# Preparing a selective scan's delta and delta u: where the copies, the constant and the units on GpSimd are put

## The chip, the cores and the metric

The kernel runs on one core of a Trainium2 chip. The metric is the device time of one launch in microseconds (us), lower is better. A core has five engines with queues of their own: TensorE (PE in the profile, with its weight loads as PEld), VectorE (DVE), ScalarE (ACT), GpSimd (POOL) and SyncE (SP), which here only issues the transfers. Each takes its instructions in order; semaphores tie them together.

## The reference

Four layers, each x + ss2d(group_norm(x)), over eight images of 48 x 48 positions and 96 channels. Of one layer, what matters here is the selective scan over 192 inner channels, 16 states and four directions (rows, columns, and both backwards):

```python
x_dbl = jnp.einsum('bkdl,kcd->bkcl', xs, x_proj_weight)
dts, Bs, Cs = jnp.split(x_dbl, [R, R + N], axis=2)
dts = jnp.einsum('bkrl,kdr->bkdl', dts, dt_projs_weight)
A = -jnp.exp(A_logs.astype(jnp.float32)).reshape(K, Din, N)
delta = jax.nn.softplus(dts + dt_projs_bias.reshape(K, Din)[None, :, :, None])
...
def step(h, inp):
    u, dl, Bv, Cv = inp
    dA = jnp.exp(dl[..., None] * A)
    h = h * dA + (dl * u)[..., None] * Bv[:, :, None, :]
    y = jnp.einsum('bkdn,bkn->bkd', h, Cv)
    return (h, y)
```

Around it stand an input projection, a depthwise 3 x 3 convolution with SiLU before, a layer norm, a gate with SiLU and an output projection behind. Layer 3 sums its decays in another way (a cumulative sum divided by the decay); the kernel gives it a short path of its own, over the ends of the sequence alone.

## The kernel before, in words

**Chunks and units.** Layers 0 to 2 run over four pairs of images, and each pair over 12 groups: three tiles of channels, two orders of the positions (ph), two directions (d). A group of 2304 positions is cut into 3 chunks of 768. That makes 432 chunks. A chunk is worked off in 16 units n; one unit has 128 partitions, which are 64 channels for each of two states. A unit needs, over its 768 positions: the decay exp(delta a), made by ScalarE (`exp`, L764); delta u times B; the scan h = decay h + delta u B on VectorE (L798); h times C on GpSimd (L807); and the sum over states on TensorE into a PSUM accumulator (`add_up`, L854).

**Two kinds of units.** In ten units of a chunk the rows of B are spread over the partitions by four bf16 matmuls from `brow` into a PSUM tile `b` of a pool of two (`spread`, L667), and VectorE multiplies them with delta u (L794) ahead of the scan. In the other six (`pooled`, L711) a transfer brings B already spread into the tile `bb`, GpSimd multiplies it with delta u (`weigh`, L741), and ScalarE's decay goes into the PSUM tile `b` instead; VectorE then has the scan alone. The transfer of `bb` is issued five turns ahead of its unit and `weigh` three.

**Delta of the next chunk.** While a chunk runs, `prepare` (L580) makes the delta of the next, in two halves of 384 positions: a matmul from the rank to the channels (L603); |x|, relu, exp(-|x|) on ScalarE (L611 to L613); ln(1 + e), 1 + e and 1 - (1 + e) (L615 to L617); and eight matmuls with identity matrices that sum e, 1 - (1 + e), the logarithm and the relu in a PSUM bank v (L623). The pair e and 1 - (1 + e) adds what 1 + e lost in rounding. Then `to_twins` (L574) copies delta from v into both halves of the partitions with four copies on ScalarE (L578), VectorE multiplies v by u in place (`times_u`, L631 or, with strided columns, L634), and four more copies take delta u out of v. Each `yield` ends a step of `prepare`, and one step is made in each turn.

**The order.** There is no scheduler: the order on each engine is that in which the loop of `run` issues. Turn k issues, for unit k: the transfers ahead, `spread` of unit k + 1 (or its exponential into PSUM), `weigh` and the exponential of unit k + 3, the copy of the last unit's carry, the product and scan of unit k, the product with C; then one step of `prepare` and one step of side work (`beside`: the convolution and projections of the next pair, or the epilogue of the last), and `add_up` of unit k - 2. When a chunk's accumulator is finished, it is copied out by ScalarE (L871), and the next one begins with four matmuls (`begin_sum`, L839) ahead of the sum of unit 1; a chunk that turns from forwards to backwards keeps its accumulator. In the turn in which an accumulator is copied out, `beside` comes before `add_up`. Two turns after a chunk's first unit no side step is made.

A `spread` needs a buffer of `b`, so it waits for the scan of two units before. TensorE takes it in order, and VectorE's product waits for it.

**Rows of B.** `load` (L743) fetches `brow`, 2 x 48 rows of bf16, with the transfers of a chunk's first unit, four turns ahead.

## Time and profile before

| | |
|---|---|
| median of 3 runs | 20515.53 us (20514.31 to 20521.39) |
| the profiled execution's own time | 20509.65 us |
| its span, first to last instruction | 20507.7 us |
| mean granted TensorE clock | 0.904 |
| busy DMA engines, 1000 to 18000 us | 0.83 to 0.87 in windows of 1000 us |
| product with C on POOL, three forms over 768 positions | 1.815 to 1.817 us |
| product with B on POOL | 1.819 us, 2592 of them |
| product with B on DVE | 0.946 us, 4320 of them |
| scan on DVE | 1.739 to 1.814 us, 6912 of them |
| exponential on ACT | 0.901 to 0.931 us, 6912 of them |
| a 64 x 384 copy on ACT | 0.473 us, 2 x 3456 of them |
| 1 - (1 + e) on ACT, L617 | 0.615 us, 864 of them over 384 positions |
| product with u on DVE | 0.543 us (L631) and 0.814 us (L634), 432 each |

A row of the profile's groups names line, engine, operation, output and inputs with shapes, count, busy time and the mean of one; "idle before" is time in which the engine stood ahead of such an instruction, with what ended it. In the view of waits each row reads: who waited, for whom, total us, times, longest. Busy times of engines that overlap say little of the end; what counts is which wait ends last. Layers 0 to 2 take the first 18500 us; layer 3's short path the rest.

### The profile page before, as it was taken

What the parts mean: (1) busy time and instruction counts of PE and PEld (TensorE: products, weight loads), DVE (VectorE), ACT (ScalarE), POOL (GpSimd) and SP (SyncE); (2) the same over time, 40 slices, a digit from 0 to 9 for tenths busy, and PEclk for the clock granted to TensorE, in tenths of its full rate; (3) what the DMA queues carried; (4) which work ended last, traced back from release to release, by engine and by line L of the source; (5) the groups of instructions that cost most, each with busy time, mean ns of one, the idle gap of its engine ahead of it and who ended that gap; (6) DMA issues with size and microseconds to landing.
All of it is one profiled execution on the core that took longest, in us unless ns stands there. A gap on an engine that the chain in (4) does not pass through costs nothing. (4 is left out here: it accounts for less than half of the span.)

```text
span 20507.7 us, 304889 instructions
## 1 busy us (share of the span) xinstructions
PE 17283.2 (84%) x88322; PEld 7546.6 (37%) x88322; DVE 17656.0 (86%) x14161; ACT 16243.7 (79%) x30020; POOL 17768.2 (87%) x10121
## 2 busy tenths in 40 slices
PE   8888888888888888888888888888888888888886
PEld 2323333333333333333333333333333333335565
DVE  5999999999999999999999999989989989995543
ACT  5777887887887887887877887877877877877776
POOL 5999999999999999999999999999999999995432
PEclk8998998998998999998998999988988998999997
DMA  5888888888888888888888888888888888883221
GB/s 147 223 221 222 219 220 224 222 219 221 220 225 222 219 229 221 221 229 219 221 228 220 217 225 219 218 218 220 217 219 219 220 219 222 219 220 109 76 72 51
DMA packets 1963444, 4200.13 MB, mean 205 GB/s; under 512 B 369456, under 2 KB 720048, under 8 KB 1948592
## 3 DMA queue, kind: packets, MB, share of 16 engines
q1 hardware_dynamic: 1961776, 4180.52, 77.8%
q8 instruction: 726, 11.89, 0.3%
q14 instruction: 942, 7.72, 0.2%
HBM read 4026.64 MB, written 152.27 MB: 204 GB/s over the span
## 5 line engine op out<-in xcount | busy, mean ns | idle before, releaser
L807 POOL TENSOR_TENSOR cb<-cb,da 128x768 f32<-128x768 f32 x4320 | 7831.3, 1817 | 799.5 <-issue 258.3
L854 PE MATMUL acc<-cb,twin 128*64 128x384 f32 x27648 | 7018.1, 542 | 663.6 <-POOL cb L807 660.3
L798 DVE TENSOR_TENSOR_SCAN da<-da,carry,b 128x768 f32<-128x768 f32 x2880 | 5223.3, 1814 | 176.4 <-ACT b L764 2.3
L741 POOL TENSOR_TENSOR bb<-bb,du 128x768 f32<-128x768 f32 x2592 | 4714.0, 1819 | 361.0 <-DMA bb<-xd 207.8
L794 DVE TENSOR_TENSOR b<-du,b 128x768 f32<-128x768 f32 x4320 | 4087.6, 946 | 883.9 <-PE b L667 785.4
L807 POOL TENSOR_TENSOR cb<-cb,bb 128x768 f32<-128x768 f32 x2592 | 4705.1, 1815 | 155.0 <-DVE bb L798 57.1
L667 PE MATMUL b<-brow,pick 96*64 96x512 bf16 (+2 forms) x18816 | 2761.6, 355 | 1787.6 <-DVE da L798 1408.4
L764 ACT ACTIVATE da<-dl,a 128x768 f32<-128x768 f32 x4320 | 4013.6, 931 | 245.8 <-POOL cb L807 214.0
L854 PEld LDWEIGHTS acc<-cb,twin 128*64 128x64 f32 x27648 | 2268.9, 150 | 3089.4 <-issue 1400.3
L798 DVE TENSOR_TENSOR_SCAN bb<-b,carry,bb 128x768 f32<-128x768 f32 x1728 | 3109.0, 1799 | 114.8 <-ACT b L764 53.5
L764 ACT ACTIVATE b<-dl,a 128x768 f32<-128x768 f32 x2592 | 2334.4, 901 | 590.2 <-DVE da L798 558.4
L798 DVE TENSOR_TENSOR_SCAN da<-da,b 128x768 f32<-128x768 f32 x1440 | 2525.4, 1754 | 85.6 <-DVE b L794 0.9
L667 PEld LDWEIGHTS <-pick 96*64 96x64 bf16 x18816 | 974.1, 114 | 4192.1 <-DVE da L798 2506.3
L578 ACT COPY dl<-ps 64x384 f32<-64x384 f32 x3456 | 1635.3, 473 | 756.7 <-PE ps L623 720.7
L312 PE MATMUL ps<-pad,diag 128*128 128x480 f32 (+1 forms) x4320 | 2165.7, 599 | 11.5 <-DVE eyc L1087 9.9
L623 PE MATMUL ps<-du,cst 128*64 128x384 f32 (+1 forms) x7296 | 1709.7, 516 | 93.1 <-ACT du L617 77.0
L578 ACT COPY du<-ps 64x384 f32<-64x384 f32 x3456 | 1635.7, 473 | 190.0 <-DVE ps L634 91.2
L798 DVE TENSOR_TENSOR_SCAN bb<-b,bb 128x768 f32<-128x768 f32 x864 | 1502.2, 1739 | 94.9 <-ACT b L764 40.5
L623 PE MATMUL ps<-dl,cst 128*64 128x384 f32 (+1 forms) x7296 | 1412.4, 483 | 0.0
L312 PEld LDWEIGHTS ps<-pad,diag 128*128 128x128 f32 x4320 | 687.5, 191 | 1211.4 <-issue 1090.1
L603 PE MATMUL ps<-dts,w 6*128 6x384 f32 (+5 forms) x2432 | 946.3, 595 | 176.1 <-DMA dts<-xd 103.7
L611 ACT ACTIVATE du<-ps,w 128x384 f32<-128x384 f32 (+1 forms) x912 | 521.4, 572 | 622.3 <-PE ps L603 611.5
(144 smaller groups left out, 19159.8 us busy)
## 6 DMA issues: line engine op xcount, KB each, us to landing
cb<-xd SPq DMA_DIRECT2D x13952, 192.0 KB
bb<-xd SPq DMA_DIRECT2D x5184, 192.0 KB
brow<-xb SPq DMA_DIRECT2D x864, 72.0 KB
yd<-y SPq DMA_DIRECT2D x48, 1152.0 KB
ey<-yd SPq DMA_DIRECT2D x256, 216.0 KB
cb<-xd SPq DMA_DIRECT2D x128, 384.0 KB
ex<-xs SPq DMA_DIRECT2D x256, 108.0 KB
xd<-xt SPq DMA_DIRECT2D x32, 684.0 KB
```

Of the source, the lines that this page charges most:

```text
L312: nc.tensor.matmul(ps[:, :m], ly.diag[:, int(t == 2), j, :], pad[:, r0 + dy : r0 + dy + nr, dx : dx + W], start=(j == 0), stop=(j == 8),)
L578: nc.scalar.copy(z[64 * h : 64 * h + 64, g, at], v[64 * g : 64 * g + 64])
L603: nc.tensor.matmul(o[:, :m], ly.dtw[q0 : q0 + r, k, chans], dts[q0 : q0 + r, at], start=True, stop=True,)
L611: nc.scalar.activation(e, v, AF.Abs, bias=bias)
L623: nc.tensor.matmul(v[half], ident[:, half], z1, start=(i == 0), stop=(i == 3))
L667: nc.tensor.matmul(o[64 * h : 64 * h + 64], pick[:, b, n : n + 1].to_broadcast([2 * NR, 64]), rows, start=True, stop=True,)
L741: nc.gpsimd.tensor_mul(b, b, self.du[n % 2])
L764: nc.scalar.activation(da, self.dl[n % 2], AF.Exp, scale=layers[self.l].a2[:, int(self.t == 2), n % 2, k, i : i + 1],)
L794: nc.vector.tensor_mul(b, self.du[n % 2], b)
L798: nc.vector.tensor_tensor_scan(way(h), way(da), way(b), start, ALU.mult, ALU.add)
L807: nc.gpsimd.tensor_mul(c, c, h)
L854: nc.tensor.matmul(self.acc[64 * g : 64 * g + 64, a, : self.m // 2], twin, c[:, a, :], start=False, stop=(pair + 2 == NS and not self.turns),)
```

## The change

It has four parts.

1. `prepare` no longer makes 1 - (1 + e) on ScalarE. A bf16 matrix with ones in its first row and zeros elsewhere, times a column of ones, puts the constant 1 in v with two matmuls over 384 columns; -(1 + e) is added by a negated identity (`less`, in the place of a constant that is no longer used by then).
2. The four copies of delta stay. `times_u` comes one turn after them, in the first half of a chunk as in the second, and writes `du` in SBUF. Three copies within SBUF then bring delta u into both halves of the partitions.
3. The units with B on GpSimd are 2, 4, 7, 9, 12 and 15 in place of 2, 5, 7, 10, 13 and 15.
4. `brow` of the next chunk is fetched in turn 6, ten units ahead, where the next chunk belongs to the same layer and pair.

```diff
+    less = cst[:, P : 2 * P]
+    unit = cpool.tile([P, 64], BF16, name="unit")
+    nc.gpsimd.memset(unit, 0.0)
+    nc.gpsimd.memset(unit[0:1], 1.0)
+    unit_row = cpool.tile([P, 1], BF16, name="unit_row")
+    nc.gpsimd.memset(unit_row, 1.0)
...
+    nc.scalar.activation(less, ident, AF.Copy, scale=-1.0)
...
-            nc.scalar.activation(w1, w1, AF.Identity, bias=ones, scale=-1.0)
             yield
             v = bank()[:, :m]
-            for i, z1 in enumerate((e, w1, lg, x)):
+            for g in range(2):
+                nc.tensor.matmul(
+                    v[64 * g : 64 * g + 64], unit, unit_row.to_broadcast([P, m]),
+                    start=True, stop=False,
+                )
+            for w, z1 in ((less, w1), (ident, e), (ident, lg), (ident, x)):
                 for g in range(2):
                     half = slice(64 * g, 64 * g + 64)
-                    nc.tensor.matmul(
-                        v[half], ident[:, half], z1, start=(i == 0), stop=(i == 3)
-                    )
-                if i % 2 == 1:
+                    nc.tensor.matmul(v[half], w[:, half], z1, start=False, stop=(z1 is x))
+                if z1 is e or z1 is x:
                     yield
...
-            to_twins(dl, at, v)
+            for g in range(2):
+                for h in range(2):
+                    nc.scalar.copy(dl[64 * h : 64 * h + 64, g, at], v[64 * g : 64 * g + 64])
             if z + m == c.m:
                 if l == NLAYER - 1:
                     c.sum_up()
                 c.ready = True
+            yield
+            times_u(du[:, 0, at])
+            yield
+            for h in (1, 0):
+                nc.scalar.copy(du[64 * h : 64 * h + 64, 1, at], du[64:P, 0, at])
+            nc.scalar.copy(du[64:P, 0, at], du[0:64, 0, at])
+            if z + m < c.m:
                 yield
-            times_u(v)
-            yield
-            to_twins(du, at, v)
-            yield
...
-            return n in (2, 5, 7, 10, 13, 15) and self.l < NLAYER - 1
+            return n in (2, 4, 7, 9, 12, 15) and self.l < NLAYER - 1
...
+            if n == 6 and coming_to < len(chunks):
+                z = chunks[coming_to]
+                if (z.l, z.p) == (l, p):
+                    z.load_rows()
```

`load_rows` holds the lines that were in `load` and returns at once where the rows have been fetched.

The steps of `prepare` fall on other turns. First half: matmuls of the sum in turns 2 and 3 as before, delta's copies in turn 4, the product with u behind unit 5 (before: unit 4), delta u's copies in turn 6 (before: 5). Second half: the matmul from the rank in turn 7 (6), the sum in 10 and 11 (9 and 10), delta's copies in 12 (11), the product with u behind unit 13 (12), delta u's copies in turn 14 (13).

More of the change, by code (lines that the diff above doesn't have):

```diff
@@ L572, in load_dt @@
             )
-    def to_twins(z, at, v):
-        for g in range(2):
-            for h in range(2):
-                nc.scalar.copy(z[64 * h : 64 * h + 64, g, at], v[64 * g : 64 * g + 64])
     def prepare(c):
@@ L741, in weigh, with load_rows @@
                 nc.gpsimd.tensor_mul(b, b, self.du[n % 2])
+        def load_rows(self):
+            if self.brow is not None:
+                return
+            self.brow = rpool.tile([2 * NR, SCAN], BF16, name="brow", tag="brow")
+            for j, b in enumerate(range(2) if self.t == 2 else (self.t, self.t)):
+                nc.sync.dma_start(
+                    self.brow[NR * j : NR * j + NR, : self.m],
+                    state[self.l, self.p]["xb"][
+                        self.ph, b, :, self.d, :, self.c0 : self.c0 + self.m
+                    ],
+                )
         def load(self, n):
-            s, m, at = state[self.l, self.p], self.m, slice(self.c0, self.c0 + self.m)
             if n == 0:
-                self.brow = rpool.tile([2 * NR, SCAN], BF16, name="brow", tag="brow")
-                for j, b in enumerate(range(2) if self.t == 2 else (self.t, self.t)):
-                    nc.sync.dma_start(
-                        self.brow[NR * j : NR * j + NR, :m],
-                        s["xb"][self.ph, b, :, self.d, :, at],
-                    )
+                self.load_rows()
             self.cb[n] = cb = cbpool.tile([P, SCAN], F32, name="cb", tag="cb")
```

## The prediction

> **What bounds the kernel now.** I read the page first (its busy line and slices), then the waits of each engine between 1000 and 18500 us, where layers 0 to 2 run, and then the timeline of one chunk.

> ```profile
> PE 17283.2 (84%) x88322; PEld 7546.6 (37%) x88322; DVE 17656.0 (86%) x14161; ACT 16243.7 (79%) x30020; POOL 17768.2 (87%) x10121
> ...
> POOL 5999999999999999999999999999999999995432
> PEclk8998998998998999998998999988988998999997
> ```

> No engine is alone at its limit. Layers 0 to 2 are 432 chunks of 16 units. From scan end to scan end in the trace, a chunk takes 42.5 us. POOL's own work for it is 16 products with C and 6 with B, 22 x 1.816 = 40.0 us; DVE's is 10 units at about 2.7 us (product and scan, back to back), 6 at 1.75 (scan alone) and two products with u (0.55 or 0.81 each), some 39 us, and about 0.7 for norms. So 3 us of a chunk are waits between engines; only these can be won or lost in layers 0 to 2. Which waits DVE has:

> ```profile
> DVE b L794 <- PE b L667: 745.4, 702, 5.9
> DVE ps L634 <- ACT dl L578: 112.7, 109, 3.6
> DVE bb L798 <- ACT b L764: 90.8, 63, 3.3
> DVE b L794 <- PE acc L854: 85.4, 34, 4.8
> DVE ps L631 <- ACT dl L578: 84.1, 94, 3.5
> ```

> The columns are total us, times, longest. The window holds 412 chunks, so DVE waits 1.8 us a chunk for TensorE's rows of B (`spread`, L667), 0.48 for ScalarE's delta copies before it may multiply by u in place (L631, L634), 0.22 for an exponential. By unit, the first kind stands before unit 11 (0.67 us a chunk on average) and unit 1 (0.50); before units 3, 4 and 6 it is under 0.15.

> The next view is TensorE's timeline where units 1 to 6 of one chunk go by:

> ```profile
> 6022.51 0.52 PE L667 MATMUL b<-brow,pick 96*64 96x512 bf16 x4
> 6022.85 0.81 PE L854 MATMUL acc<-cb,twin 128*64 128x384 f32 x4
> 6023.50 1.46 PE L623 MATMUL ps<-du,cst 128*64 128x384 f32 x8
> 6024.79 0.49 PE L667 MATMUL b<-brow,pick 96*64 96x512 bf16 x4
> 6025.12 1.46 PE L623 MATMUL ps<-dl,cst 128*64 128x384 f32 x8
> 6026.51 1.04 PE L465 MATMUL ps<-u,w 64*96 64x480 f32 x2
> 6027.48 1.51 PE L839 MATMUL acc<-y,cst 128*64 128x384 f32 x8
> 6028.82 1.46 PE L854 MATMUL acc<-cb,twin 128*64 128x384 f32 x8
> 6030.11 0.50 PE L667 MATMUL b<-brow,pick 96*64 96x512 bf16 x4
> ```

> The three L667 rows are B of units 3, 4 and 6. Between the first and the last TensorE never rests: a sum, delta's matmuls, a side matmul, the start of the next accumulator (L839), two sums. This is the densest stretch of a chunk. DVE beside it:

> ```profile
> 6025.98 0.94 DVE L794 TENSOR_TENSOR b<-du,b 128x768 f32<-128x768 f32 x1
> 6027.02 1.81 DVE L798 TENSOR_TENSOR_SCAN da<-da,carry,b 128x768 f32<-128x768 f32 x1
> 6028.89 0.83 DVE L634 TENSOR_TENSOR ps<-ps,u 128x384 f32<-128x384 f32 x1
> 6029.64 1.80 DVE L798 TENSOR_TENSOR_SCAN bb<-b,carry,bb 128x768 f32<-128x768 f32 x1
> 6031.37 0.93 DVE L794 TENSOR_TENSOR b<-du,b 128x768 f32<-128x768 f32 x1
> ```

> Unit 4, the product with u, unit 5 (scan alone: its B was weighed on POOL), unit 6. DVE needs TensorE's next rows only at 6031.4, and they are there. Unit 5 and the product with u are the cover of TensorE's burst.

> [...] a sum's matmul takes 493 ns at full and 830 at half clock, half clock holds 48% of unit 0's time and 42% of unit 1's, and of 128 chunks with over 0.4 us of wait before unit 1, the stretch before was at half clock for 89%. [...] the trace has 0.474 for the latter, and for activations over 128 partitions 0.605 from SBUF (L616) against 0.580 from PSUM (L611).

> **The change, part by part.**

> *1 - (1 + e) on TensorE.* ScalarE loses L617, 0.615 us a half chunk, 1.23 a chunk. TensorE gains two bf16 matmuls over 384 columns. The 768 columns of a `spread` take 0.33 us from issue to issue (6022.51 to 6022.85), so half of that, 0.17 us a half chunk. They stand ahead of delta's other matmuls and need no ScalarE result, but whatever follows them is 0.17 later. TensorE waited 218 us for L617 in the whole trace, 0.25 a half chunk; its idle inside the burst above is only 0.1 us on average, so I count no gain from this.

> *Delta u into SBUF, the copies apart.* The product with u reads PSUM and writes SBUF; I take its time as unchanged (0.543, 0.814), bounds -0.05 and +0.05 a half. It no longer overwrites what ScalarE still copies, so DVE's 0.48 us a chunk go. ScalarE makes 3 copies for 4: [...] In all ScalarE is freed of 2 us a chunk; it is not the bound (79%), so this pays only where it is waited for: the 0.22 for exponentials, of which I take 0.1. The preparation takes one turn more: the second half's copies of delta u come in unit 14, not 13. What waits for them is POOL's product with B of the next unit 2, in turn 15 behind the product of unit 14; ScalarE finishes some 3.5 us after scan 13 (exponentials of 15 and 17, then three copies), POOL arrives 5.2 after it. Cover 1.7 us: no cost; without cover some 0.5 a chunk.

> *Other units on POOL.* (2, 5, 7, 10, 13, 15) becomes (2, 4, 7, 9, 12, 15), and the product with u moves from behind unit 4 to behind unit 5. The counts stay: 6 and 10. What changes is DVE's cover of the burst. B of unit 4 needs no rows any more; B of unit 5 does, and in TensorE's order its `spread` stands behind the whole burst, ahead of the second of the two sums at 6028.82. Averaged over the 350 of 420 chunks that start an accumulator: scan 1's end to the `spread` of unit 3 is 0.50 us, then 0.40, 2.16 and 4.91 to that sum, 7.97 in all. Less the `spread` of unit 4 (0.33), plus the constant row (0.17), plus 0.56 from a `spread`'s start to the product that waits for it (another in this stretch: 6001.06 to 6001.62) is 8.37. DVE gets there after units 2, 3 and 4: 1.78 + 2.86 + 1.75 = 6.39. It waits 1.98 us; in the 70 chunks that keep their accumulator, nothing. A mean of 1.65 us, low bound 1.0 (full clock, and a side step less), high 2.2. The 0.2 before unit 6 goes: DVE reaches it 3.4 us after unit 5 now (unit 5 and the product with u), and TensorE has one sum and a side matmul to do in between.

> At unit 11 the wait had another cause: in 168 of 420 chunks TensorE stood 1.9 us for POOL's product of unit 7, which the product with B of unit 10 delays, and the rows of unit 11 were behind. The same figure returns at unit 13 (POOL: B of 12 ahead of the product of unit 9). As DVE is later by then, POOL is less behind; of 0.7 I take 0.3 as left, bounds 0.1 and 1.1. Gain 0.4.

> The half clock before unit 1 stays: units 13 and 14 still give TensorE little, and now no unit on POOL shortens that stretch; +0.1, bounds -0.2 and +0.3.

> *Rows of B ten units ahead.* TensorE waited 162.5 us for them in the window, 0.4 a chunk; DVE's mean wait before unit 0 is 0.1, which goes. SyncE issues the same transfers, six turns earlier; the slot is long free.

> Sum a chunk: +1.65 +0.1 -0.2 -0.48 -0.1 -0.4 -0.1 = +0.47 us, times 432 = +203 us. Layer 3 loses 48 ScalarE instructions of about 0.44 us, and setup gains a few small ones: -10 at most. The profiled execution took 20509.65 us (span 20507.7); the median of the runs is 20515.5, so the two agree within 0.03%. Forecast 20515 + 195 = 20710, slower by 0.9%.

> **The rivals.**

> *Faster.* Place: the wait before unit 5. POOL has 1.8 us of backlog there, so DVE may wait without starving it; what counts is whether DVE makes the time up before POOL runs dry (units 8 and 14). If the wait is worth only its low bound, 1.0, and all of the 0.7 at unit 11 goes, the sum is -0.5 us, -215 us: 20300. The point from which it decides is a wait of about 1.2 us at unit 5. For it: POOL's six extra products now fall so that it is dry at one point instead of four (units 1, 6, 9, 14). Against: DVE's cycle with the 1.65 in it is 41.4 us and 0.7 of norms, before any other wait.

> *Slower by more.* Half clock falls into the burst (19% of unit 2's time now): a burst at half clock costs 4 us more, and TensorE's stretch before unit 15 is emptier. With the high bounds, 2.2 at unit 5, 1.1 at unit 13, +0.3 at unit 1: +2.0 us, +870 us; halfway, 20950.

> *No change.* ScalarE's 2 us and the wait at unit 5 cancel: 20515.

> **How the numbers follow.** Forecast (20560 to 20830) 0.43, slower by more 0.15, no change 0.08, faster 0.34. Runs of this kernel agree within some hundredths of a per cent; 0.2% (41 us) is what I call no change. Slower by over 0.2%: 0.58; within: 0.08; faster: 0.34. The range cuts the far ends of both sides: 20230 to 21100; the forecast case alone spans 20560 to 20830.

> **What would show it.** Right: in the waits of the changed kernel DVE's L-line of the product with B still waits most for `spread`, over 745 us, and by unit the largest wait stands before unit 5; the waits of the product with u for ScalarE are gone; ScalarE's busy time falls by about 0.9 ms; `spread` waits for the rows hardly at all. Wrong: a wait before unit 5 under 1 us, or DVE's sum of waits for TensorE below 745 us; then POOL's share rises over 88% and the time falls.

## The result, and the profile after

The changed kernel takes 20967.98 us (median; 20958.81 to 21012.78) against 20515.47: a ratio of 1.0224, 95% interval 1.0207 to 1.0242. It is slower by 452 us, where 195 were forecast. The place of the loss was right; two terms of the sum, the wait before unit 13 and the half clock, were too small.

The page of the changed kernel:

```profile
PE 17869.7 (85%) x90146; PEld 7759.4 (37%) x90146; DVE 17638.2 (84%) x14161; ACT 15511.5 (74%) x28247; POOL 17778.3 (85%) x10124
...
PEclk8888888888988898898898898888888888988997
```

ScalarE is relieved as counted (16243.7 to 15511.5 us busy), GpSimd's and VectorE's work is what it was, and their shares fall: the added time is waiting. TensorE's clock shows more eights (mean granted clock 0.877, before 0.904). VectorE's waits between 1000 and 18500 us, in the columns of before:

```profile
DVE b L809 <- PE b L675: 1509.7, 924, 7.1
...
DVE du L637 <- ACT dl L653: 14.9, 9, 1.7
```

The products with u (L634 and L637 here; L634 has no such wait in the window) wait for ScalarE 14.9 us in place of 196.8: that part did what was counted. But the wait for the rows of B (L675, `spread`) doubled, from 745.4 to 1509.7 us.

One chunk shows how. TensorE's timeline in the changed kernel, from delta's sum in turn 2 to turn 9:

```profile
4550.06 0.33 PE L621 MATMUL ps<-unit_row,unit 128*64 128x384 bf16 x2
4550.22 1.46 PE L628 MATMUL ps<-du,cst 128*64 128x384 f32 x8
4551.51 1.46 PE L628 MATMUL ps<-dl,cst 128*64 128x384 f32 x8
4552.90 1.02 PE L472 MATMUL ps<-u,w 64*76 64x480 f32 x2
4553.85 1.51 PE L854 MATMUL acc<-y,cst 128*64 128x384 f32 x8
4555.19 0.81 PE L869 MATMUL acc<-cb,twin 128*64 128x384 f32 x4
4555.84 0.50 PE L675 MATMUL b<-brow,pick 96*64 96x512 bf16 x4
...
4562.41 0.76 PE L675 MATMUL b<-brow,pick 96*64 96x512 bf16 x4 [2.06 <-DVE da L813]
4562.95 1.49 PE L869 MATMUL acc<-cb,twin 128*64 128x384 f32 x4
4564.38 1.54 PE L604 MATMUL ps<-dts,w 6*64 6x384 f32 x4
...
4569.14 0.61 PE L675 MATMUL b<-brow,pick 96*64 96x512 bf16 x4
```

VectorE beside it, the scans of units 3 and 4 and what follows; the bracket is the wait and what ended it:

```profile
4550.62 1.81 DVE L813 TENSOR_TENSOR_SCAN da<-da,carry,b 128x768 f32<-128x768 f32 x1
4552.35 1.79 DVE L813 TENSOR_TENSOR_SCAN bb<-b,carry,bb 128x768 f32<-128x768 f32 x1
4556.38 0.96 DVE L809 TENSOR_TENSOR b<-du,b 128x768 f32<-128x768 f32 x1 [2.24 <-PE b L675]
4557.38 1.81 DVE L813 TENSOR_TENSOR_SCAN da<-da,carry,b 128x768 f32<-128x768 f32 x1
4559.10 0.53 DVE L634 TENSOR_TENSOR du<-ps,u 128x384 f32<-128x384 f32 x1
...
4569.80 0.96 DVE L809 TENSOR_TENSOR b<-du,b 128x768 f32<-128x768 f32 x1 [1.32 <-PE b L675]
```

Busy us in four stretches of the same 20 us, then TensorE's granted clock and the share of DMA:

```profile
4550.00:4556.40 6.40, 6.40 (x40) 2.59 (x38) 4.13 (x4) 5.90 (x12) 5.20 (x4) 1.00 0.81 214
4556.40:4560.40 4.00, 3.95 (x20) 1.10 (x16) 3.96 (x4) 1.21 (x5) 2.61 (x2) 1.00 0.68 205
4560.40:4563.20 2.80, 0.79 (x6) 0.59 (x8) 2.76 (x3) 2.73 (x6) 2.80 (x3) 0.88 0.82 185
4563.20:4570.20 7.00, 7.00 (x22) 1.35 (x18) 5.65 (x5) 5.50 (x12) 6.54 (x4) 0.56 0.87 226
```

The rows of unit 5 (4555.84) stand behind the whole burst; VectorE has done unit 4's scan at 4554.1 and waits 2.24 us. With the burst over, TensorE is ahead of its work and rests 2.06 us until a buffer of `b` comes free (third stretch). Then it runs at half clock: 1.54 us for the matmul from the rank, 1.49 for a sum that took 0.81. Its work of turns 7 and 8 becomes late, and VectorE waits again, 1.32 us before unit 10. So the wait before unit 10 follows from TensorE's rest behind the burst; e3 below shows that a long wait before unit 5 is not needed for it.

The next table has all chunks of the runs: the mean of VectorE's idle time ahead of a unit's product with B, in us ("scan only" marks a unit whose B is weighed on GpSimd; slightly negative means are the overlap of records). The last column is the share of the time of units 8 and 9 in which TensorE was granted half clock.

| kernel | time, us | unit 1 | 5 | 6 | 10 | 11 | 13 | half clock |
|---|---|---|---|---|---|---|---|---|
| before | 20515 | 0.50 | scan only | 0.13 | scan only | 0.67 | scan only | 0.21 |
| changed | 20968 | 0.78 | 1.62 | -0.08 | 0.41 | -0.04 | 0.85 | 0.60 |
| e1, old units | 20171 | 0.68 | scan only | 0.38 | scan only | 0.10 | scan only | 0.24 |
| e2, new units alone | 20771 | 0.75 | 0.40 | -0.08 | -0.04 | 0.43 | -0.02 | 0.32 |
| e3, no start of the sum | 20673 | 0.83 | 0.35 | -0.08 | 0.51 | 0.03 | 1.12 | 0.61 |
| e5b, filled | 20660 | 0.40 | 1.63 | -0.08 | -0.06 | -0.04 | 0.92 | 0.17 |
| e11, 5 back | 20679 | 0.65 | scan only | 0.33 | 0.12 | 0.04 | 1.49 | 0.29 |
| e12, 10 and 13 back | 20662 | 0.64 | 1.68 | -0.08 | scan only | 0.07 | scan only | 0.53 |
| e15, B of 12 a turn later | 20371 | 0.98 | scan only | 0.38 | 0.14 | 0.03 | 0.27 | 0.26 |

### The profile page after: what moved, and what is told of

It reads as the page before. It is cut to its first block, busy times and chain, and to the rows that moved or that the text cites. A ratio compares the mean times of both kernels' runs of the same rounds, so it can differ in the third digit from the quotient of the medians.

```text
span 21011.0 us, 306251 instructions
## 1 busy us (share of the span) xinstructions
PE 17869.7 (85%) x90146; PEld 7759.4 (37%) x90146; DVE 17638.2 (84%) x14161; ACT 15511.5 (74%) x28247; POOL 17778.3 (85%) x10124
## 4 chain that ended last, share of the span: by engine, by line
PE 46%; DVE 26%; DMA 11%; issue 7%; ACT 5%; POOL 3%; SPq 2%; DVEq 0%; POOLq 0%; ACTq 0%
DVE da L813 14%; PE acc L869 12%; DVE b L809 8%; PE ps L628 8%; DMA cb<-xd 6%; PE b L675 6%; PE ps L319 5%; PE ps L604 3%; PE acc L854 3%; DMA bb<-xd 3%; POOL cb L822 2%; SPq L732 2%; PE ps L472 2%; DVE bb L813 2%; DVE du L637 1%
## 5 line engine op out<-in xcount | busy, mean ns | idle before, releaser
L869 PE MATMUL acc<-cb,twin 128*64 128x384 f32 x27648 | 7215.4, 562 | 421.5 <-POOL cb L822 414.8
L749 POOL TENSOR_TENSOR bb<-bb,du 128x768 f32<-128x768 f32 x2592 | 4706.2, 1816 | 599.0 <-DMA bb<-xd 369.0
L675 PE MATMUL b<-brow,pick 96*64 96x256 bf16 (+2 forms) x18816 | 2806.4, 365 | 2187.3 <-DVE da L813 2058.0
L675 PEld LDWEIGHTS <-pick 96*64 96x64 bf16 x18816 | 976.7, 116 | 4684.3 <-DVE da L813 3053.9
L319 PE MATMUL ps<-pad,diag 128*128 128x480 f32 (+1 forms) x4320 | 2208.2, 609 | 4.5 <-DVE du L637 2.7
L628 PE MATMUL ps<-dl,cst 128*64 128x384 f32 (+1 forms) x7296 | 1542.8, 490 | 0.0
L628 PE MATMUL ps<-du,cst 128*64 128x384 f32 (+1 forms) x7296 | 1373.1, 490 | 10.1 <-ACT du L617 10.1
L604 PE MATMUL ps<-dts,w 6*128 6x384 f32 (+5 forms) x2432 | 1121.9, 699 | 142.8 <-DMA dts<-xd 139.9
L662 ACT COPY du<-du 64x384 f32<-64x384 f32 x1728 | 882.7, 511 | 22.5 <-DVE du L634 0.6
```

The lines of the kernel that those rows point to most:

```text
L319: nc.tensor.matmul(ps[:, :m], ly.diag[:, int(t == 2), j, :], pad[:, r0 + dy : r0 + dy + nr, dx : dx + W], start=(j == 0), stop=(j == 8),)
L604: nc.tensor.matmul(o[:, :m], ly.dtw[q0 : q0 + r, k, chans], dts[q0 : q0 + r, at], start=True, stop=True,)
L628: nc.tensor.matmul(v[half], w[:, half], z1, start=False, stop=(z1 is x))
L662: nc.scalar.copy(du[64 * h : 64 * h + 64, 1, at], du[64:P, 0, at])
L675: nc.tensor.matmul(o[64 * h : 64 * h + 64], pick[:, b, n : n + 1].to_broadcast([2 * NR, 64]), rows, start=True, stop=True,)
L749: nc.gpsimd.tensor_mul(b, b, self.du[n % 2])
```

## The experiments

Edits are against the changed kernel unless the kernel before is named. Each ratio is to the kernel before, run on the same chip.

**e1, the old units with the other three parts.**

```diff
-            return n in (2, 4, 7, 9, 12, 15) and self.l < NLAYER - 1
+            return n in (2, 5, 7, 10, 13, 15) and self.l < NLAYER - 1
```

> The changed kernel with the units of before on GpSimd (2, 5, 7, 10, 13, 15); the other three parts stay. Theory A (the units decide: unit 5 had covered TensorE's burst): DVE reaches unit 6 after unit 5 and the product with u again, so the 1.62 us of wait before unit 5 go and none of that size stands elsewhere; the 0.48 us for ScalarE's copies and the waits for rows stay away: 20050 to 20350, faster than before. Theory B (TensorE's two extra matmuls, the copies one turn later or the early rows decide): most of the 452 us stay, 20850 to 21000.

20170.56 us, ratio 0.9842 (0.9825 to 0.9858): theory A, and faster than before. VectorE's waits in e1:

```profile
DVE b L809 <- PE b L675: 764.2, 606, 5.3
```

The sum is that of before again (745), but it stands elsewhere: the wait before unit 11 is 0.10 us in place of 0.67, those before units 1 and 6 are longer. Old units do not bring the wait before unit 11 back. The units cost 797 us on top of the three parts, and the three parts gain 342 without them.

**e2, the new units alone**, in the kernel before.

> The kernel before with the new units (2, 4, 7, 9, 12, 15) alone. Theory A: the wait before unit 5 comes, though smaller than 1.62 us, since the product with u (0.55 or 0.81 us) still stands ahead of it and no constant row does: about 0.8 us; with the waits at 10 and 13 some 20700 to 21000, slower than before. Theory B: within 0.3% of before, 20450 to 20580.

20770.94 us, ratio 1.0128 (1.0111 to 1.0145). The side is A's. Of the wait, only 0.40 us stands before unit 5 itself; the rest stands just ahead, at the product with u behind unit 4, which waits for delta's copies and they for TensorE's burst:

```profile
DVE ps L634 <- ACT dl L578: 269.6, 204, 5.0
DVE ps L631 <- ACT dl L578: 235.2, 181, 4.3
```

Together 1.2 us a chunk, against 0.48 before. The waits before units 10 and 13, which theory A expected too, do not come (-0.04 and -0.02 us), and 0.43 us stay before unit 11. In the changed kernel these two waits need the other parts of the change as well as the new units.

**e3 and e4, the burst made shorter.** The four matmuls that begin an accumulator are left out, and with them u's skip and the sum so far:

```diff
-                    nc.tensor.matmul(
-                        self.acc[at, a, : self.m // 2], w[:, at], self.y_part(z)[:, a],
-                        start=True, stop=False,
-                    )
...
-                    start=False, stop=(pair + 2 == NS and not self.turns),
+                    start=(pair == 0 and not self.turned), stop=(pair + 2 == NS and not self.turns),
```

> The changed kernel without the four matmuls that begin an accumulator (the skip of u and the sum so far are left out of y), 1.34 us of TensorE's burst in 5 of 6 chunks. Theory A (the burst is on the path before unit 5): the wait before unit 5 falls from 1.62 to about 0.6 us, time by 1.0 us a chunk: 20450 to 20600. Theory B (TensorE's burst is hidden): less than 100 us gained.

> The kernel before without the same four matmuls. Theory A: unit 5 and the product with u cover the burst already, only 0.13 us of wait stands before unit 6: at most 100 us gained, 20410 to 20520. Theory B (the removal helps whatever the units are, through TensorE's load): the same gain as in the changed kernel.

e3: 20672.98 us, 295 less than the changed kernel; e4: 20448.69, 64 less than before (ratio 0.9971, 0.9961 to 0.9981). The same matmuls cost nearly five times as much where no cover stands beside them: A against B. The wait before unit 5 fell from 1.62 to 0.35 us, more than expected, but the time by 0.68 us a chunk only, and e3 stays above its range: the waits before 10 and 13 grew to 0.51 and 1.12. Half clock in units 8 and 9 stayed (0.61, changed kernel 0.60), so it does not hang on how long VectorE waited before unit 5.

**e5b and e6b, TensorE's rests filled.** Three matmuls of constants, read by nobody, at the end of turns 6 and 14 (e6b: the kernel before, turn 14 alone):

```diff
+            if l not in short and n in (6, 14):
+                warm = bank()
+                for _ in range(3):
+                    nc.tensor.matmul(warm[:, : 2 * P], ident, cst[:, : 2 * P], start=True, stop=True)
```

> The changed kernel with three fp32 matmuls of constants over 256 columns, into a bank that nobody reads, at the end of turns 6 and 14, where TensorE is busy for 1.3 of 3.35 and 1.2 of 3.3 us. Theory A (TensorE's rest there brings the half clock of units 7 to 10 and 15 to 1, and this the waits before units 10 and 1, 0.41 and 0.78 us): half clock in units 8 and 9 falls from 0.6 to under 0.2, the two waits lose 0.6 us a chunk or more together, 20650 to 20800; the wait before unit 5 stays at 1.6. Theory B (the waits at 10 and 1 are TensorE's load, the clock is beside the point): the added 1.3 us of matmuls make it slower, 20970 to 21300.

> The kernel before with the same matmuls at the end of turn 14 alone. Theory A: half clock in units 15 to 1 falls from 0.3 to 0.5 to under 0.15, and the wait before unit 1 from 0.50 to 0.1 us: 20250 to 20420, faster than before. Theory B: same or slower, 20500 to 20750.

e5b: 20660.43 us, 308 less than the changed kernel, for more work on TensorE. Half clock in units 8 and 9 falls from 0.60 to 0.17, the wait before unit 10 goes, that before unit 1 halves, that before unit 5 stays. The whole window from 1000 to 18500 us, changed kernel and then e5b (PE's busy us first, PEclk third from the end):

```profile
1000.00:18500.00 17500.00, 14965.28 (x74319) 6108.53 (x74320) 15510.96 (x11687) 13042.90 (x23730) 15803.58 (x8956) 0.88 0.85 215
```

```profile
1000.00:18500.00 17500.00, 15481.54 (x80784) 6743.09 (x80782) 15811.21 (x11927) 13252.45 (x24212) 16133.36 (x9151) 0.95 0.86 219
```

e6b: 20427.84, ratio 0.9962 (0.9948 to 0.9976), 80 us gained and the wait before unit 1 down from 0.50 to 0.17. The time is 8 us outside theory A's range: other waits took some 0.14 us of the 0.33.

**e8b, the same filling on e1.**

> The other three parts of the change with the units of before, and the matmuls of constants at the end of turns 6 and 14. Theory A: half clock in units 15 to 1 (0.22 to 0.37) goes, and most of the wait before unit 1, 0.68 us, with it: 19850 to 20050. Theory B: 20170 to 20450.

20175.12 us, no gain (e1: 20170.56), against the expectation. Half clock is gone (0.05 of the time for 0.13) and the wait before unit 1 falls from 0.68 to 0.44 us, but 0.15 to 0.2 us each come up before units 0 and 8, where TensorE has the filling behind it. TensorE is busier here than in e5b (15685 against 15482 of the 17500 us); that it is too full for the filling is likely, but not shown.

**e7b, the rows late again.**

```diff
-            if n == 6 and coming_to < len(chunks):
-                z = chunks[coming_to]
-                if (z.l, z.p) == (l, p):
-                    z.load_rows()
```

> The changed kernel without its fourth part: rows of B are fetched four units ahead again. Theory C (the transfers of the rows, now in turn 6, make the B of unit 12 late, for which POOL waits 0.68 us and TensorE after it, so that DVE waits 0.85 before unit 13): the waits before bb of unit 12 and before unit 13 lose half or more, POOL waits before unit 2 instead, 20750 to 20900. Theory D (they are late since TensorE's burst holds the sums that free the buffers): the wait before unit 13 stays, DVE waits some 0.1 to 0.2 us more at unit 0: 20980 to 21080.

20914.77 us, 53 less than the changed kernel and between the two ranges. The runs of the two kernels do not overlap (20914 to 20933, 20959 to 21013), though the intervals of their ratios do (1.0182 to 1.0216, 1.0207 to 1.0242). GpSimd's wait for the B of unit 12 falls from 0.68 to 0.08 us and stands before unit 2 instead (0.08 to 0.42); the wait before unit 13 falls from 0.85 to 0.56. C holds for a third of that wait, and D's share is not excluded.

**e11 and e12, the units one place at a time**: (2, 5, 7, 9, 12, 15) and (2, 4, 7, 10, 13, 15).

> The changed kernel with unit 5 on GpSimd in place of unit 4, the others as changed (2, 5, 7, 9, 12, 15). Theory A (the cover of the first burst is the larger part, with the half clock behind it): the wait before unit 5 (1.62) and that before unit 10 (0.41) go, that before unit 13 (0.85) stays: 20250 to 20500. Theory E (9 and 12 in place of 10 and 13 are what costs): 20800 to 20970.

> The changed kernel with units 10 and 13 back, and 4 kept: (2, 4, 7, 10, 13, 15). Theory A: the wait before unit 5 stays at 1.6 and the half clock of units 7 to 10 with it, the wait before unit 13 goes, the one before 10 too, since it has no rows: 20650 to 20900. Theory E: 20170 to 20350.

20678.87 and 20661.57 us: 289 and 306 gained, where undoing both gains 797. e12 lies in A's range, at its low end, and its wait before unit 5 and the half clock stay as A said, with a wait of 0.32 us before unit 9 added. e11 lies in neither range: the wait before unit 5 is gone, but the one before unit 13 grows to 1.49 us. The two stand in for each other: with the wait before unit 5, GpSimd's product of unit 9 ends 4.76 us after its scan, without it 5.71 us, so GpSimd works off arrears while VectorE waits, and unit 13 has less to wait for.

GpSimd in e11, from the product with C of unit 8 to those of 10 and 11:

```profile
5533.79 1.82 POOL L822 TENSOR_TENSOR cb<-cb,da 128x768 f32<-128x768 f32 x1
5537.73 1.81 POOL L749 TENSOR_TENSOR bb<-bb,du 128x768 f32<-128x768 f32 x1 [2.12 <-DMA bb<-xd]
5539.50 1.83 POOL L822 TENSOR_TENSOR cb<-cb,bb 128x768 f32<-128x768 f32 x1
5541.29 3.58 POOL L822 TENSOR_TENSOR cb<-cb,da 128x768 f32<-128x768 f32 x2
```

and TensorE, which stands before the sum that needs the product of unit 9:

```profile
5541.79 0.87 PE L869 MATMUL acc<-cb,twin 128*64 128x384 f32 x4
5542.48 1.46 PE L628 MATMUL ps<-dl,cst 128*64 128x384 f32 x8
5543.87 1.07 PE L319 MATMUL ps<-pad,diag 128*128 128x480 f32 x2
5544.88 0.52 PE L675 MATMUL b<-brow,pick 96*64 96x512 bf16 x4
```

The product with B of unit 12 (L749) waits 2.12 us for its transfer, the product of unit 9 (5539.50) comes behind it, the sum at 5541.79 behind that, then half of delta's sum and a side matmul, and only then the rows of unit 13. VectorE waits 1.44 us for these.

**e13 and e15, what holds up the product of unit 9.** e13 is e11 with the rows late; e15 is e11 with `weigh` of unit 12 one turn later, behind the product of unit 9:

```diff
-            early(DECAYS, "weigh")
+            for i in range(0 if k == 0 else k + 1, min(k + DECAYS + 1, len(todo))):
+                _, z, zn = todo[i]
+                if k == 0 or (i == k + 1) == (zn == 12):
+                    z.weigh(zn)
```

> Units (2, 5, 7, 9, 12, 15) with the other parts of the change but the rows four units ahead. Theory C (the rows' transfers make B of unit 12 late): POOL's wait before it falls from 0.98 to about 0.1 us and the wait before unit 13 from 1.49 to under 0.6: 20350 to 20500. Theory F (the order on POOL makes it): the wait before unit 13 stays over 1.0, as POOL comes from further behind: 20600 to 20700.

> Units (2, 5, 7, 9, 12, 15) with all other parts, and POOL's product with B of unit 12 one turn later, behind the product with C of unit 9. Theory F (the product of unit 9, which the sum before unit 13 needs, is held up by the product with B ahead of it, transfer and all): the wait before unit 13 falls from 1.49 to under 0.4 us: 20200 to 20400. Theory C alone would give the same only through the transfer: POOL's wait for B of 12 goes, but 0.5 us or more of the wait before 13 stay: 20400 to 20550.

e13: 20549.13 us, 130 less than e11 and between the two ranges; GpSimd waits 0.12 us for its B in place of 0.98, VectorE 0.92 before unit 13 in place of 1.49. e15: 20370.66, 308 less; 0.27 us before unit 13. So with the other parts in place the wait needs the order on GpSimd (F), and the early rows' transfers (C) add a good third of it. The order alone does not make it: e2 has the same order and no wait before unit 13.

**e9, e10 and e14, the parts that gain.** With the old units: part two alone; parts one and two; parts two and four.

> The kernel before with the second part alone (product with u a unit after delta's copies, delta u into SBUF, three copies). Theory A (the step later moves the second sum of delta away from TensorE's wait for the product of unit 7, and DVE no longer waits for the copies, 0.48 us a chunk): nearly all of the 342 us that the three parts gain with the old units, 20170 to 20300. Theory B (ScalarE's relief by the constant row or the early rows share it): 20330 to 20450.

> Parts one and two with the old units, the rows of B four units ahead. Theory A (the early rows are worth the 0.1 us before unit 0, as counted): 20190 to 20240. Theory C (in turn 6 they delay B on POOL, as they did in the changed kernel, where undoing them gained 53 us): 20100 to 20170.

> Parts two and four with the old units, 1 - (1 + e) on ScalarE again. By the runs so far part two alone is 20233, parts one and two 20273, one, two and four 20170: if the parts add up, 20130, which would be the fastest; if ScalarE's relief is needed for the early rows to pay, 20170 to 20250.

| parts with the old units | time, us | ratio to before |
|---|---|---|
| 2 | 20233.39 | 0.9866 (0.985 to 0.9883) |
| 1 and 2 | 20273.37 | 0.9891 (0.9875 to 0.9908) |
| 1, 2 and 4 (e1) | 20170.56 | 0.9842 (0.9825 to 0.9858) |
| 2 and 4 (e14) | 20145.62 | 0.9829 (0.9813 to 0.9845) |

The copies carry the gain, 265 us (theory A of e9). The early rows give 90 to 100 more with the old units, twice what was counted: the expectation of e10 fell on both theories. The constant row gives nothing: 25 and 40 us slower with it, each pair within its intervals. e14, 16 us above the sum of its parts and below the other case, is the fastest version found, 1.7% below before. Its VectorE waits for ScalarE's copies are nearly gone as well and its main wait, for the rows of B, is shorter than that of before (714.5 us in the window, 745.4 before).

## Why the prediction was right in its direction and wrong in its size

Point by point, a chunk, in us:

| step | forecast | measured |
|---|---|---|
| wait before unit 5 | +1.65 (1.0 to 2.2) | +1.62 |
| product with u waits for the copies | -0.48 | 196.8 to 14.9 us in the window, -0.44 |
| before unit 6 | -0.2 | 0.13 to -0.08, -0.21 |
| before unit 0, rows | -0.1 | 0.12 to -0.06, -0.17 |
| unit 11, returning at 13 | 0.7 to 0.3, -0.4 | 0.67 to 0.85, +0.14 |
| half clock, before unit 1 | +0.1 | 0.50 to 0.78, +0.29 |
| half clock, before unit 10 | not listed | +0.41 |
| exponentials | -0.1 | 90.8 to 64.4 us in the window, -0.06 |
| sum; measured: all of VectorE's idle time | +0.47 | 3.69 to 4.91, +1.22 |

**Right.** The burst of TensorE was read off the timeline of before with its length, and the wait that it leaves when unit 4 takes unit 5's place came out within 0.03 us. e1 shows that the units made the loss, e3 and e4 that the burst is what unit 5 covered. That the mean came out so close is in part luck. In the chunks that start an accumulator, unit 5's product began 8.39 us after unit 1's scan (8.37 forecast), but VectorE was there after 6.61 (6.39 forecast) and waited 1.77 us, not 1.98; in the 72 chunks that keep theirs it waited 0.87, not nothing. The prices held: the constant row delays what follows by 0.16 us (4550.06 to 4550.22; 0.17 taken), a copy within SBUF takes 0.511 us (L662), one from PSUM 0.474 (L578 of before), so three for four save ScalarE 0.36 us a half and 1.95 a chunk with the 1.23 of L617, where the author's estimate was 2.

**Wrong: the term of unit 13.** The prediction took the wait before unit 11 for one that GpSimd's units make and that returns before unit 13 as 0.3 us, "as DVE is later by then, POOL is less behind". The run measured 0.85. VectorE's wait does let GpSimd catch up (e11 without it: 1.49), but two things were left out. The first is a wait of GpSimd itself: 0.68 us for the B of unit 12, to which the change's own early rows, counted as free of cost, add (e7b, e13). The second is part two, which moves delta's sum and the product with u one turn later. The new units alone keep the wait before unit 11 and make none before unit 13 (e2: 0.43 and -0.02); the other parts with the old units remove the one before unit 11 (e1: 0.10). e2 and e7b have the same units and late rows, and GpSimd's product of unit 9 ends as late after its scan (4.20 and 4.17 us). In e2 the rows of unit 13 begin 1.08 us before the end of unit 12's scan, and the product with u stands ahead of unit 13's product. In e7b, with the later steps, they begin 0.33 us before it, nothing stands between, and the wait is 0.56 us. So the wait comes of the order on GpSimd together with these steps; how much each of them has in it is not separated, nor is the constant row's share, which e7b has too.

**Wrong: the clock.** The prediction named half clock before unit 1 and gave it +0.1; it gave units 7 to 10 nothing. It counted what VectorE waits for, and not what the new order leaves TensorE to do: unit 5's rows stand last in the burst, so VectorE begins unit 5 when the burst is over, and TensorE has little work while VectorE makes units 5 and 6. In unit 6 it is busy 1.31 of 3.35 us (before: 2.28 of 2.95). This is a matter of the order and not of the wait's length: in e3, with 0.35 us of wait before unit 5, it is still 1.31 of 3.36. Part two has a share here too. In e2 the matmul from the rank still stands in turn 6 and the product with u behind unit 4; TensorE is busy 1.67 of 2.73 us in unit 6, and half clock in units 8 and 9 is 0.32. That little work of TensorE goes with half clock behind it was the author's estimate for unit 1. The traces show it there (before: 1.19 of 2.72 us busy in unit 14, 0.34 of unit 15 at half clock; changed: 1.16 of 3.32, and 0.44) and here as well: half clock in units 8 and 9 rose from 0.21 to 0.60. e5b fills the rests and takes 308 us less.

With these two terms as measured (+0.54 for unit 13, +0.60 for the clock) the sum would have been 1.6 us a chunk. The trace has 1.17 (42.49 to 43.66 from scan end to scan end; the profiled execution is the slowest of the four, and the median's 452 us are 1.05). The difference of some 0.4 us is in VectorE's shorter idle times, which the list lacks: in units 7, 8 and 12 they fall by 0.12, 0.07 and 0.10, and in unit 10 the wait for rows takes the place of 0.22 us ahead of its scan. The case named "slower by more" has 20950, close to the result, but that is in part luck. Of its causes a wait at unit 13 near 1.1 (0.85) and +0.3 at unit 1 (+0.29) came; a burst at half clock, its first, did not (half clock in unit 3 stayed at 0.06), nor did 2.2 at unit 5, and unit 10 is not in it. One reading of the prediction is mixed, without effect on the sum: TensorE's waits for L617 are 223 us in the whole trace, not 218.

## What to carry to other kernels

In a schedule written out by hand, ask of every move not only what it takes off an engine but what it uncovers: list the longest stretch in which an engine cannot rest, and which work of its reader stands beside it. Ask too what the new order leaves the engine to do behind its burst: here TensorE had 1.31 us of work in the 3.35 us of unit 6, and 0.60 of units 8 and 9 ran at half clock. A step moved by one turn can decide where a wait stands, as those of part two did for units 10, 11 and 13. When two changes of order are made together, try each alone; here each undone alone gave under 40% of what both gave.
